# A graph layer and a mixture of experts on one core: thirteen experts' weights ahead instead of eleven, and a rearranged start and end of the expert loop

## The chip, the cores and the metric

The kernel runs on one core of a Trainium2 chip. Its time is the device time of one execution in microseconds (us), taken as the median of several runs; one further execution is recorded by the hardware profiler, and all views of the profile come from that one. Engines are named as the profile names them: PE (TensorE matmul), PEld (its weight load), DVE (VectorE), ACT (ScalarE), POOL (GpSimd) and SP (SyncE, which here only issues transfers). ACT and POOL issue transfers too.

## The reference

There are 1,024 nodes of 512 features, all in float32, and 16,384 edges sorted by target.

1. Graph layer: `x = x + relu(segment_sum(edge_weight * (layernorm(x) @ W)[src], dst) + bias)`.
2. Experts: `x' = layernorm(x)` is this layer's input; `scores = sigmoid(x' @ Wg.T + bg)`, and `nx` is `x'` normalised once more. The two best of 64 experts are taken, their scores divided by their sum.
3. Each expert computes `h = silu((nx*gamma_e + beta_e) @ W1_e + b1_e)`, times `(nx*gamma_e + beta_e) @ W3_e + b3_e` (512 to 256), then `h @ W2_e + b2_e` (256 to 512), weighted with the score. With W1, W3 and W2 an expert has three weight matrices of 524,288 B each, 64 experts together some 100 MB.
4. A shared expert of width 32 is applied to every node, and everything is added to `x`.

## The kernel before

**Graph stage.** The edges are turned into a dense matrix by one-hot matmuls (`one_hots`, `matrix_group`, `turn`), and `weighted_sum` (L507, 128 matmuls of 128x512) multiplies it with the normalised features times W. Tile by tile (8 tiles of 128 nodes) the stage normalises, stores the twice normalised rows to `nx_d` in device memory (`store_nx`, L539, on ACT's queue), transposes (`turn_x`), computes the scores (`scores`, L551, L554), takes the two best (`choose`, L560 to L572), counts each token's rank within its expert (`rank`, `put`, L588 to L598), and places token numbers in the lists of 32 pairs of experts with 64 places for each expert (`slots`, `listed`, L607 to L615). `lists` and `tokens` (L691, L692) come last.

**Blocks.** After that there are 33 blocks: one for every pair of experts (64 rows each), and at position 24 one overflow block for the tokens of an expert beyond its 64 places. Blocks are numbered 0 to 32 in the order they run. Each block does:

- `fetch`: POOL gathers 128 rows from `nx_d` (L717), up to four blocks ahead, in `NR` = 4 buffers that POOL zeroes first (L713);
- `front`: PE transposes them (L194), DVE applies gamma and beta (`scaled`, L729, L731);
- `hidden`: four bias matmuls (L742; b1 and b3 split into three bf16 terms, high and middle in `bias_hm`, low in `bias_lo`), sixteen matmuls with W1 and W3 (L746), Silu on ACT (L749), product on DVE (L751);
- `turned`: two transposes (L758) and a copy (L760);
- `back`, one block later: eight matmuls with W2 (`outputs`, L768), a copy on ACT (L771), and a scatter of 128 rows to `y_d` (L775, POOL).

The order of each engine's instructions is that of the program text (`manual_schedule`). Other work is put between the blocks: `beyond` and `beyond_list` work out the overflow block (blocks 2 to 11), and `other_rows`, `other_turn`, `other_sum` compute the shared expert and the b2 terms of one tile of nodes (L885 to L908): tiles 0 and 1 ahead of the loop, tiles 2 to 7 from block 13 on. `weights` (L791 to L798) normalises the scores and stores them to `w_d` (L795, on ACT's queue); it stands ahead of the loop.

**Weights.** `load_expert` issues W1, W3 (L703, L704, into one 8 KB slot per partition, tag `w13`) and W2 (L706, a 4 KB slot, tag `w2`) on SP's queue. There are `AHEAD` = 11 slots of each tag. The same slots serve the graph stage as temporary storage (`big` and `mid` tiles), and its end serves them again (`ys`, `bhots`, `diag`). Loads are issued in program order as slots come free. All transfers that SP and ACT issue share eight completion semaphores, taken in turn in the order of the program: a transfer waits on its queue until the one eight places ahead in that list has landed, whichever of the two queues that one is on.

**Pools.** The small tiles of the graph stage are in pools of their own (`gp`, `gp2`, `rt`); when these close, the pools of the blocks (`bp`, `gb`, `lp`, `psx`) take the same memory, and their first users wait for everything that used the closed pools.

**End.** When the scatter of block 31 has landed, eight loads (L1006, 512 KB each, alternately on ACT's and SP's queue) fetch `y_d`. The last block isn't scattered: PE adds its rows by one-hot matmuls (L1010), and one of the two rows of every odd tile by a diagonal matmul (L1012). DVE adds the rest (multiply-add L1014, sum L1016), and eight stores write the result (L1017).

The function and the loop around the change are these:

Of the kernel before, what the change touches and what calls it, by code (L numbers as in the profile page):

```python
# [18 lines left out]
P = 128  # L19
EPS = 1e-5  # L20
AHEAD = 11
# [3 lines left out]
def kernel(  # L25
# [111 lines left out]

    bias_hm = const.tile([P, 2 * H], BF16, name="bias_hm")
    bias_lo = const.tile([E, 2 * H], BF16, name="bias_lo")
    both = const.tile([P, E], BF16, name="both")  # L140
# [59 lines left out]
    with tc.tile_pool(name="graph", bufs=1) as gp, \  # L200
            tc.tile_pool(name="graph2", bufs=2) as gp2, \
# [5 lines left out]
        def row_tile(name):  # L207
            return gp2.tile([P, D], F32, name=name, tag="row", bufs=6)

        with tc.manual_schedule(engines={ENG.PE, ENG.DVE, ENG.Activation, ENG.Pool}):  # L210

            nc.gpsimd.iota(iota, pattern=[[1, P]], base=0, channel_multiplier=0, allow_small_or_imprecise_dtypes=True)
            thr_row = gp.tile([P, NH, P], F32, name="thr_row")
# [5 lines left out]
            diff = gp.tile([P, P], F32, name="diff")  # L219
# [32 lines left out]
            below = gp.tile([P, NH, P], BF16, name="below")  # L252
# [8 lines left out]
            rows = gp.tile([P, NH, EJ], I32, name="erows")  # L261
# [24 lines left out]
            def turn_h(i):  # L286
                pt = pst.tile([P, KC, P], F32, name="pt")
                transpose_rows(pt, hs.pop(i), P)
                hTs[i] = gp2.tile([P, KC, P], F32, name="hT")
                nc.scalar.copy(hTs[i], pt)  # L290
# [16 lines left out]
            sm = gp.tile([P, NH, EJ], F32, name="sm")  # L307
# [7 lines left out]
            d_w = gp.tile([P, NH, P], I32, name="d_w")  # L315
            s_w = gp.tile([P, NH, P], I32, name="s_w")
            e_w = gp.tile([P, NH, P], F32, name="e_w")
# [18 lines left out]
            b13 = mid([P, 2, H], "b13", F32)  # L336
            for n in range(2):
                nc.gpsimd.dma_start(b13[n * E:(n + 1) * E, 0, :], b1)
                nc.gpsimd.dma_start(b13[n * E:(n + 1) * E, 1, :], b3)
# [29 lines left out]
            blk_i = gp.tile([P, NH, P], I32, name="blk_i")  # L369
            nc.vector.tensor_scalar(blk_i, d_w, 2, None, op0=ALU.logical_shift_right)  # L370
            nc.vector.tensor_scalar(d_w, d_w, DL - 1, None, op0=ALU.bitwise_and)
            hi_i = gp.tile([P, NH, P], I32, name="hi_i")
            nc.vector.tensor_scalar(hi_i, s_w, 6, None, op0=ALU.logical_shift_right)
            nc.vector.tensor_scalar(s_w, s_w, LO - 1, None, op0=ALU.bitwise_and)
            part = gp.tile([P, 3, NH, P], F32, name="part")
# [39 lines left out]
            row_a = gp.tile([P, P], I32, name="row_a")  # L415
            nc.vector.tensor_scalar(row_a, at_i, 3, None, op0=ALU.logical_shift_right)
            nc.vector.tensor_scalar(row_a, row_a, 7, None, op0=ALU.bitwise_and)
            row_b = gp.tile([P, P], I32, name="row_b")
# [18 lines left out]
        with tc.If(unsure):  # L437
            for h in range(NH):
                nc.sync.dma_start(hw_d[h * D:(h + 1) * D, :].rearrange("(i p) d -> p i d", p=P), hws[h])
            bias_sb = row_tile("bias_sb")[:1, :]  # L440
            nc.sync.dma_start(bias_sb, gnn_bias[None, :])
# [4 lines left out]
            for b in range(NT // 2):  # L446
                node = row_tile("node")
# [27 lines left out]
        with tc.manual_schedule(engines={ENG.PE, ENG.DVE, ENG.Activation, ENG.Pool}):  # L475
# [35 lines left out]
            xts, xtTs, ohots, picked, ranks, earlier, bases, shifts = {}, {}, {}, {}, {}, {}, {}, {}  # L511
# [29 lines left out]
            def turn_x(t):  # L541
                pt = pst.tile([P, KC, P], F32, name="pt")
                transpose_rows(pt, xts.pop(t), P)
                xtTs[t] = gp2.tile([P, KC, P], F32, name="hT")
                nc.scalar.copy(xtTs[t], pt)

            def scores(t):
                pl = psh.tile([P, D], F32, name="ph")[:, :P]
                nc.tensor.matmul(pl, ones[0:1, :], brow, start=True, stop=False)
# [7 lines left out]
            def choose(t):  # L557
# [17 lines left out]
                earlier[t + 1] = to  # L575

# [8 lines left out]
            def put(t):  # L585
# [4 lines left out]
                odd_i = rt.tile([P, 2], U32, name="odd_i")  # L590
                nc.vector.tensor_scalar(odd_i, idx[:, t, :2], 1, None, op0=ALU.bitwise_and)
                pair_i = rt.tile([P, 2], U32, name="pair_i")
                nc.vector.tensor_scalar(pair_i, idx[:, t, :2], 1, None, op0=ALU.logical_shift_right)
                nc.vector.tensor_copy(pair[:, t, :], pair_i)
# [30 lines left out]
            def bias_terms():  # L625
                v = b13.rearrange("p a h -> p (a h)")
                terms = [mid([P, 2 * H], "bterm", BF16) for _ in range(2)]
                for term in terms:
                    nc.vector.tensor_copy(term, v)
                    nc.vector.tensor_sub(v, v, term)  # L630
# [28 lines left out]
            for t in range(NT + 4):  # L659
# [18 lines left out]
                if have(1):  # L678
                    turn_x(t - 1)
# [391 lines left out]
```

## Time and profile before

| | us |
|---|---|
| median of 3 runs | 466.25 |
| lowest, highest | 465.24, 466.73 |
| profiled execution, its time | 467.33 |
| profiled execution, its span | 465.5 |
| PE busy | 422.5 (91%) |
| DVE busy | 233.5 |
| POOL busy | 116.2 |
| ACT busy | 112.0 |
| moved by transfers | 132.48 MB, of which 107.56 on SP's queue |

The span is the stretch that the profiler saw; the time is that of the same execution as the runs are timed. Busy times are of the whole span and lump together stages with different limits, so they have to be read by stage. In a timeline the columns are start, duration, engine, line, operation, tiles (out<-in), count, and in brackets the idle time of the engine before it and what ended it. An engine's name with a q (SPq, ACTq) is the issue of a transfer.

### The profile page before, as it was taken

The numbers are of one execution on the slowest core, as the hardware profiler recorded it, in microseconds if no ns is written. First come the engines' busy times: TensorE is split into PE (matmuls) and PEld (weight loads), VectorE is DVE, ScalarE is ACT, GpSimd is POOL, SyncE is SP. The second block draws the span as 40 slices with busy tenths as digits, with TensorE's granted clock in tenths as the row PEclk, the third lists the DMA queues.
The fourth block names the chain that finished last, engine by engine and source line by source line (L and its number), as shares of the span: only waits on it lengthen the run. The fifth ranks groups of instructions, "written<-read, shape, count | busy, mean of one in ns | idle before, by whom it ended". The sixth has DMA issues, their size and how long they took to land. (4 is left out here: it accounts for less than half of the span.)

```text
span 465.5 us, 6433 instructions
## 1 busy us (share of the span) xinstructions
PE 422.5 (91%) x2182; PEld 210.6 (45%) x2182; DVE 233.5 (50%) x690; ACT 112.0 (24%) x240; POOL 116.2 (25%) x148
## 2 busy tenths in 40 slices
PE   2999999987999964996999999999999999999781
PEld 1554996754555543332434434333333443434230
DVE  6879996036877875428424333233233232412265
ACT  1335785324121212011111212112121121212200
POOL 6542200000432124312223233232232322200200
PEclk9999999998999985799899999999999999999988
DMA  8286830360786195359999999999999999999194
GB/s 263 87 121 102 321 130 3 125 259 28 244 316 204 52 375 195 121 194 410 356 389 407 407 407 406 407 408 405 408 404 409 406 405 407 405 410 403 47 366 174
DMA packets 42294, 132.48 MB, mean 285 GB/s; under 512 B 8023, under 2 KB 8151, under 8 KB 42128
## 3 DMA queue, kind: packets, MB, share of 16 engines
q1 hardware_dynamic: 30464, 107.56, 59.7%
q0 software_dynamic: 8304, 18.17, 13.3%
q10 hardware_dynamic: 3488, 6.30, 3.7%
q8 instruction: 18, 0.29, 0.3%
q14 instruction: 20, 0.16, 0.1%
HBM read 124.00 MB, written 18.88 MB: 307 GB/s over the span
## 5 line engine op out<-in xcount | busy, mean ns | idle before, releaser
L746 PE MATMUL xph<-w,xT 128*64 128x512 f32 (+1 forms) x520 | 126.5, 602 | 0.9 <-DMA w<-in_L_ffn_W_dram 0.9
L775 POOL DMA_INDIRECT y_d<-xy,lists x31 | 31.9, 1030 | 169.8 <-ACT xhT L760 70.4
L746 PEld LDWEIGHTS xph<-w,xT 128*64 128x64 f32 (+1 forms) x520 | 39.0, 138 | 66.6 <-issue 63.6
L768 PE MATMUL xpy<-w,xhT 128*64 128x512 f32 (+1 forms) x260 | 67.0, 593 | 0.6 <-ACT xhT L760 0.6
L751 DVE TENSOR_TENSOR xh<-xa,xph 128x256 f32<-128x256 f32 x33 | 13.9, 421 | 106.8 <-ACT xa L749 106.8
L507 PE MATMUL acc<-hw,AT 128*128 128x512 f32 x128 | 61.5, 607 | 0.0
L749 ACT ACTIVATE xa<-xph 128x256 f32<-128x256 f32 x33 | 12.6, 383 | 152.1 <-PE xph L746 152.1
L717 POOL DMA_INDIRECT rows<-nx_d,tokens x32 | 35.5, 1109 | 12.4 <-issue 9.1
L768 PEld LDWEIGHTS xpy<-w,xhT 128*64 128x64 f32 (+1 forms) x260 | 21.5, 138 | 37.2 <-issue 35.1
L485 PEld LDWEIGHTS ph<-oh 128*64 128x64 f32 x512 | 31.7, 212 | 5.7 <-issue 3.3
L485 PE MATMUL ph<-oh 128*64 128x64 f32 x512 | 33.3, 302 | 0.1
L297 PE MATMUL ph<-w_sb,hT 128*128 128x512 f32 x64 | 30.5, 625 | 0.7 <-ACT hT L290 0.7
L771 ACT COPY xy<-xpy 128x512 f32<-128x512 f32 x33 | 19.3, 586 | 49.0 <-PE xpy L768 44.1
L729 DVE TENSOR_TENSOR xT<-xpt,gT 128x512 f32<-128x512 f32 x32 | 22.0, 687 | 16.7 <-PE xpt L194 15.3
L507 PEld LDWEIGHTS acc<-hw,AT 128*128 128x128 f32 x128 | 22.3, 193 | 17.4 <-issue 17.4
L731 DVE TENSOR_TENSOR xT<-xT,bT 128x512 f32<-128x512 f32 x32 | 22.2, 693 | 1.1
L607 POOL TENSOR_SCALAR so<-rank_at,here 128x128 f32<-128x128 f32 x14 | 8.9, 634 | 54.5 <-DVE here L598 54.5
L194 PE MATMUL xpt<-ident,rows 128*128 128x128 f32 x132 | 22.3, 296 | 0.0
L401 DVE TENSOR_TENSOR oh<-eq,wt 128x1024 f32<-128x1024 bf16 x16 | 19.6, 1224 | 3.6 <-PE pt L498 2.2
L194 PEld LDWEIGHTS xpt<-ident,rows 128*128 128x128 f32 x132 | 19.5, 211 | 1.1 <-issue 0.6
L758 PEld LDWEIGHTS xpht<-ident,xh 128*128 128x128 f32 x66 | 11.8, 216 | 16.1 <-DVE xh L751 7.0
L297 PEld LDWEIGHTS ph<-w_sb,hT 128*128 128x128 f32 x64 | 12.4, 203 | 14.1 <-issue 13.1
(275 smaller groups left out, 493.9 us busy)
## 6 DMA issues: line engine op xcount, KB each, us to landing
w<-in_L_ffn_W_dram SPq DMA_DIRECT2D x195, 512.0 KB
y_d<-zero POOLq DMA_DIRECT2D x1, 4096.0 KB
base_d<-in_L_gnn_bias_dram POOLq DMA_DIRECT2D x1, 2048.0 KB, 19.9
base<-base_d POOLq DMA_DIRECT2D x8, 256.0 KB, 13.3
nx_d<-nx ACTq DMA_DIRECT2D x8, 256.0 KB
ys<-y_d ACTq DMA_DIRECT2D x4, 512.0 KB
ys<-y_d SPq DMA_DIRECT2D x4, 512.0 KB
w_sb<-in_L_gnn_W_dram ACTq DMA_DIRECT2D x1, 1024.0 KB
```

Of the source, the lines that this page charges most:

```text
L194: nc.tensor.transpose(ps[:, k, :], v[:, k, :], ident[:n, :n])
L297: nc.tensor.matmul(ph, hT[:, k, :], w_sb[:, k, :], start=(k == 0), stop=(k == KC - 1))
L401: nc.vector.tensor_tensor(oh[:, 1], eq[:, 1], wt[:, h, None, q].to_broadcast([P, LO, 16]), ALU.mult)
L485: nc.tensor.matmul(pa[LO * w:LO * (w + 1), u, :], oh[:, 1, :, q], oh[:, 0, :, q], start=True, stop=True)
L507: nc.tensor.matmul(accs[t], ATs[h][t // 4][:, t % 4, wq, :], hws[h][:, wq, :], start=(h == 0 and wq == 0), stop=(h == NH - 1 and wq == NQ ...
L717: nc.gpsimd.indirect_dma_start(out=rows, out_offset=None, in_=nx_d[:, :], in_offset=bass.IndirectOffsetOnAxis(ap=of, axis=0), bounds_check ...
L729: nc.vector.tensor_tensor(xT.rearrange(view, n=n), pt.rearrange(view, n=n), g[:, :, :, None].to_broadcast(over), ALU.mult)
L731: nc.vector.tensor_tensor(xT.rearrange(view, n=n), xT.rearrange(view, n=n), b[:, :, :, None].to_broadcast(over), ALU.add)
L746: nc.tensor.matmul(ph[n * r:(n + 1) * r], xT[:, k, n * r:(n + 1) * r], w13[:, :, k, :], start=False, stop=(k == KC - 1))
L768: nc.tensor.matmul(py[n * r:(n + 1) * r], hT[:, c, n * r:(n + 1) * r], w2[:, c, :], start=(c == 0), stop=(c == HC - 1))
L771: nc.scalar.copy(y, py)
L775: nc.gpsimd.indirect_dma_start(out=y_d[:, :], out_offset=bass.IndirectOffsetOnAxis(ap=numbers, axis=0), in_=y, in_offset=None, bounds_chec ...
```

## The change

- `AHEAD` goes from 11 to 13. The memory for it comes from the graph stage: its row tiles, turned tiles, early tiles and edge windows now lie in ring slots (`mid`, `big`), `beyond` keeps its tables in a `w2` slot (`room`), and several block tiles have fewer buffers (`xT` 2, `xa1`, `xh`, `xhT` and `st` 1, `xy` 2, `rows` 3).
- The bias is kept as three bf16 terms of 32 experts in one tile of 96 partitions per half (`bias3`, `picks`): a pair's block issues two bias matmuls instead of four. The tile is loaded by twelve small transfers on POOL instead of four.
- The blocks' pools wait tile by tile (`reuse_waits="tile"`), not for the whole closed pools.
- In the graph stage `score_bias` comes ahead of `turn_x`, and the two parity operations of `put` move to `choose`.
- The row buffers are zeroed by ACT. Three gathers are issued ahead of `front(0)`, the fourth after it.
- `weights()` moves from ahead of the loop to block 0, behind its `hidden`; the shared-expert work of all eight tiles moves into blocks 6 to 29.
- The last pair's loads come in the order W1, W3 of both experts, then W2 of both.
- The end: the last two blocks aren't scattered. The eight loads of `y_d` are all on SP's queue, directly behind the last weight loads. PE adds both blocks by one-hot matmuls, and the diagonal matmul is left for the last two tiles; the steps on DVE are in another order.

The core of the diff:

```diff
-AHEAD = 11
+AHEAD = 13
...
-    bias_hm = const.tile([P, 2 * H], BF16, name="bias_hm")
-    bias_lo = const.tile([E, 2 * H], BF16, name="bias_lo")
-    both = const.tile([P, E], BF16, name="both")
+    EH = E // 2
+    bias3 = const.tile([3 * EH, 2, 2 * H], BF16, name="bias3")
+    picks = const.tile([3 * EH, 2, E], BF16, name="picks")
...
-        def row_tile(name):
-            return gp2.tile([P, D], F32, name=name, tag="row", bufs=6)
+        row_ring = [pair[:, j] for pair in [mid([P, 2, D], "row", F32) for _ in range(3)] for j in range(2)]
+        turned_ring = mid([P, 2, KC, P], "hT", F32)
+        taken = {"row": 0, "turned": 0}
+        def row_tile(name=None):
+            taken["row"] += 1
+            return row_ring[taken["row"] % len(row_ring)]
+        def turned_tile():
+            taken["turned"] += 1
+            return turned_ring[:, taken["turned"] % 2]
...
-            b13 = mid([P, 2, H], "b13", F32)
-            for n in range(2):
-                nc.gpsimd.dma_start(b13[n * E:(n + 1) * E, 0, :], b1)
-                nc.gpsimd.dma_start(b13[n * E:(n + 1) * E, 1, :], b3)
+            b13 = mid([3 * EH, 2, 2, H], "b13", F32)
+            for n in range(3):
+                for a in range(2):
+                    for m, of in enumerate((b1, b3)):
+                        nc.gpsimd.dma_start(b13[n * EH:(n + 1) * EH, a, m, :], of[a * EH:(a + 1) * EH, :])
...
+            def score_bias(t):
+                pls[t] = psh.tile([P, D], F32, name="ph")[:, :P]
+                nc.tensor.matmul(pls[t], ones[0:1, :], brow, start=True, stop=False)
...
+                odds[t] = rt.tile([P, 2], U32, name="odd_i")
+                nc.vector.tensor_scalar(odds[t], idx[:, t, :2], 1, None, op0=ALU.bitwise_and)
+                pair_i = rt.tile([P, 2], U32, name="pair_i")
+                nc.vector.tensor_scalar(pair_i, idx[:, t, :2], 1, None, op0=ALU.logical_shift_right)
+                nc.vector.tensor_copy(pair[:, t, :], pair_i)
...
-                v = b13.rearrange("p a h -> p (a h)")
-                terms = [mid([P, 2 * H], "bterm", BF16) for _ in range(2)]
-                for term in terms:
-                    nc.vector.tensor_copy(term, v)
-                    nc.vector.tensor_sub(v, v, term)
-                nc.vector.tensor_copy(bias_hm[:E, :], terms[0][:E, :])
-                nc.vector.tensor_copy(bias_hm[E:, :], terms[1][E:, :])
-                nc.vector.tensor_copy(bias_lo, v[:E, :])
-                nc.vector.tensor_add(both, ident[:, :E], ident[:, E:])
+                terms = mid([3 * EH, 2, 2 * H], "bterm", BF16)
+                v = b13.rearrange("p a m h -> p a (m h)")
+                for n in range(3):
+                    part = slice(n * EH, (n + 1) * EH)
+                    nc.vector.tensor_copy(terms, v)
+                    nc.vector.tensor_copy(bias3[part], terms[part])
+                    if n < 2:
+                        nc.vector.tensor_sub(v, v, terms)
+                nc.vector.memset(picks, 0.0)
+                for n in range(3):
+                    part = slice(n * EH, (n + 1) * EH)
+                    for a in range(2):
+                        nc.vector.tensor_copy(picks[part, a, a * EH:(a + 1) * EH], ident[part, part])
...
+                    score_bias(t - 1)
...
-    bp = ctx.enter_context(tc.tile_pool(name="block", bufs=3))
-    gb = ctx.enter_context(tc.tile_pool(name="rows", bufs=1))
-    lp = ctx.enter_context(tc.tile_pool(name="late", bufs=1))
-    psx = ctx.enter_context(tc.tile_pool(name="ps_x", bufs=2, space=bass.MemoryType.PSUM))
-    def load_expert(queue, w1_of, w3_of, w2_of):
+    gb = ctx.enter_context(tc.tile_pool(name="rows", bufs=1, reuse_waits="tile"))
+    bp = ctx.enter_context(tc.tile_pool(name="block", bufs=3, reuse_waits="tile"))
+    lp = ctx.enter_context(tc.tile_pool(name="late", bufs=1, reuse_waits="tile"))
+    psx = ctx.enter_context(tc.tile_pool(name="ps_x", bufs=2, space=bass.MemoryType.PSUM, reuse_waits="tile"))
...
-    NR = 4
-    for rows in rows_of:
-        nc.gpsimd.memset(rows, 0.0)
+    NR = 3
...
-        for terms in (bias_hm, bias_lo):
-            rows = terms.shape[0]
+        for a in range(2):
             for n, (_, pick) in enumerate(parts):
-                nc.tensor.matmul(ph[n * r:(n + 1) * r], pick[:rows].to_broadcast([rows, r]), terms,
-                                 start=(terms is bias_hm), stop=False)
+                if a in pick:
+                    nc.tensor.matmul(ph[n * r:(n + 1) * r], pick[a].to_broadcast([3 * EH, r]), bias3[:, a, :],
+                                     start=(a == min(pick)), stop=False)
...
+        room = wpool.tile([P, 16, E], F32, name="room", tag="w2")
...
     with tc.manual_schedule(engines={ENG.PE, ENG.DVE, ENG.Activation, ENG.Pool, ENG.SP}):
-        for n in range(4):
+        for rows in rows_of:
+            nc.scalar.activation(rows, ones[:, 0:1].to_broadcast([P, D]), AF.Copy, scale=0.0)
+        for n in range(NR):
             fetch(n)
-        weights()
-        sts = [other_rows(i) for i in range(2)]
-        sTs = [other_turn(st) for st in sts]
-        for i in range(2):
-            other_sum(i, sTs[i])
         front(0)
+        fetch(NR)
         front(1)
         hots, st, sT = None, None, None
         for n, q in enumerate(order):
             if q < NP:
-                parts = [(load_expert(nc.sync, W1[e:e + 1], W3[e:e + 1], W2[e:e + 1]), both[:, e:e + 1])
-                         for e in (2 * q, 2 * q + 1)]
+                both = (2 * q, 2 * q + 1)
+                if n < LAST:
+                    experts = [load_expert(nc.sync, W1[e:e + 1], W3[e:e + 1], W2[e:e + 1]) for e in both]
+                else:
+                    experts = list(zip([load_first(nc.sync, W1[e:e + 1], W3[e:e + 1]) for e in both],
+                                       [load_second(nc.sync, W2[e:e + 1]) for e in both]))
+                parts = [(of, {e // EH: picks[:, e // EH, e:e + 1]}) for of, e in zip(experts, both)]
             else:
                 e = nc.values_load(oexp_i[0:1, 0:1], engines=[ENG.SP], min_val=0, max_val=E - 1)
-                parts = [(load_expert(nc.sync, W1[ds(e, 1)], W3[ds(e, 1)], W2[ds(e, 1)]), pick_o)]
+                parts = [(load_expert(nc.sync, W1[ds(e, 1)], W3[ds(e, 1)], W2[ds(e, 1)]), either)]
             fetch(n + 4)
+            if n == LAST:
+                y_of = y_d.rearrange("(i p n) d -> i p n d", p=P, n=2)
+                ys = [wpool.tile([P, 2, 2, D], F32, name="ys", tag="w13")[:, j] for i in range(NT // 2) for j in range(2)]
+                for i in range(NT):
+                    nc.sync.dma_start(ys[i], y_of[i])
+                hots_last = [block_hots(tokens[:, NP - 2 + m:NP - 1 + m], w_last[m]) for m in range(2)]
+                diag = wpool.tile([P, 2, P], F32, name="diag", tag="w2")
+                for j in range(2):
+                    nc.scalar.activation(diag[:, j, :], ident, AF.Copy, scale=wts[:, NT - 2 + j, 1:2])
             h = hidden(xTs.pop(n), parts)
-            back(n - 1)
+            if n < LAST:
+                back(n - 1)
+            else:
+                y_last = [outputs(*hTs.pop(LAST - 1))]
+            if n == 0:
+                weights()
             if n == 2:
                 beyond()
             if 4 <= n < 4 + NT:
             if n == 4 + NT:
                 beyond_lists()
-            if n >= 13 and (n - 13) // 3 + 2 < NT:
-                i = (n - 13) // 3 + 2
-                if n % 3 == 1:
+            if n >= 6 and (n - 6) // 3 < NT:
+                i = (n - 6) // 3
+                if n % 3 == 0:
                     st = other_rows(i)
-                elif n % 3 == 2:
+                elif n % 3 == 1:
                     sT = other_turn(st)
                 else:
                     other_sum(i, sT)
-            if n == LAST - 1:
-                w_last = block_weights(lists[:, NP - 1:NP])
-                hots_last = block_hots(tokens[:, NP - 1:NP], w_last)
-                diag = wpool.tile([P, NT // 2, P], F32, name="diag", tag="w2")
-                for i in range(1, NT, 2):
-                    nc.scalar.activation(diag[:, i // 2, :], ident, AF.Copy, scale=wts[:, i, 0:1])
+            if n == LAST - 2:
+                w_last = [block_weights(lists[:, NP - 2 + m:NP - 1 + m]) for m in range(2)]
             hTs[n] = (turned(h), parts)
             front(n + 2)
-        y_of = y_d.rearrange("(i p n) d -> i p n d", p=P, n=2)
-        queues = (nc.scalar, nc.sync)
-        ys = []
-        for i in range(NT):
-            ys.append(wpool.tile([P, 2, D], F32, name="ys", tag="w13"))
-            queues[i % 2].dma_start(ys[i], y_of[i])
-        y = outputs(*hTs.pop(LAST))
-        for i in range(NT):
-            po = psx.tile([P, D], F32, name=("xpt", "xph", "xpy")[i % 3])
-            nc.tensor.matmul(po, hots_last[:, i, :], y, start=True, stop=(i % 2 == 0))
-            if i % 2:
-                nc.tensor.matmul(po, diag[:, i // 2, :], ys[i][:, 0, :], start=False, stop=True)
-            for n in range(i % 2, 2):
+        pos = {}
+        def add_block(m, i):
+            if m == 0:
+                pos[i] = psx.tile([P, D], F32, name=("xpt", "xph", "xpy", "xpht")[i % 4])
+            nc.tensor.matmul(pos[i], hots_last[m][:, i, :], y_last[m], start=(m == 0), stop=(m == 1))
+            if m == 0 and i >= NT - 2:
+                nc.tensor.matmul(pos[i], diag[:, i - NT + 2, :], ys[i][:, 1, :], start=False, stop=False)
+        def add_rows(i):
+            for n in range(2 if i < NT - 2 else 1):
                 nc.vector.scalar_tensor_tensor(res[:, i, :], ys[i][:, n, :], wts[:, i, n:n + 1], res[:, i, :],
                                                op0=ALU.mult, op1=ALU.add)
-            nc.vector.tensor_add(res[:, i, :], res[:, i, :], po)
+        def add_sums(i):
+            nc.vector.tensor_add(res[:, i, :], res[:, i, :], pos.pop(i))
             queues[i % 2].dma_start(out[i * P:(i + 1) * P, :], res[:, i, :])
+        queues = (nc.scalar, nc.sync)
+        add_block(0, 0)
+        y_last.append(outputs(*hTs.pop(LAST)))
+        add_block(0, 1)
+        for i in range(2):
+            add_rows(i)
+        for i in range(NT):
+            add_block(1, i)
+            if i + 2 < NT:
+                add_block(0, i + 2)
+                add_rows(i + 2)
+            add_sums(i)
```

## The prediction

> **What bounds the kernel now.** I read the page's head first, then the waits of SP's queue, the issue rows on SP, the windows by stage, and the rows at the two joints: routing to block 0, and last block to the end.
>
> From the page:
>
> ```profile
> span 465.5 us, 6433 instructions
> ...
> PE 422.5 (91%) x2182; PEld 210.6 (45%) x2182; DVE 233.5 (50%) x690; ACT 112.0 (24%) x240; POOL 116.2 (25%) x148
> ...
> GB/s 263 87 121 102 321 130 3 125 259 28 244 316 204 52 375 195 121 194 410 356 389 407 407 407 406 407 408 405 408 404 409 406 405 407 405 410 403 47 366 174
> ```
>
> PE looks like the bound at 91%. But a slice is 11.6 us, and from slice 21 to slice 36 the transfers stand on a plateau of about 407 GB/s. The waits of the SP queue (line, what ended the wait, us in total, times, longest) say who is late:
>
> ```profile
> SPq L706 <- DMA w<-in_L_ffn_W_dram: 35.3, 36, 1.5
> ...
> SPq L703 <- DMA w<-in_L_ffn_W_dram: 32.9, 34, 1.4
> ...
> SPq L706 <- DMA nx_d<-nx: 23.0, 1, 23.0
> SPq L703 <- PE xph L746: 20.8, 1, 20.8
> ...
> SPq L1006 <- DMA y_d<-xy,lists: 17.7, 1, 17.7
> ```
>
> Weight loads wait for earlier weight loads. One waited 23.0 us for a store that ACT issued: a load on SP waits for whichever transfer, on SP or ACT, stands eight places ahead in one common list. And one waited 20.8 us for a matmul of block 0, a ring slot. Its place, and two windows (PE, PEld, DVE, ACT, POOL busy, granted PE clock, DMA share, GB/s):
>
> ```profile
> 172.91 0.33 SPq L706 DMA_DIRECT2D w<-in_L_ffn_W_dram  x1
> 194.91 0.33 SPq L703 DMA_DIRECT2D w<-in_L_ffn_W_dram  x1
> ```
>
> ```profile
> 180.00:195.00 15.00, 11.93 (x38) 5.56 (x38) 7.34 (x26) 2.21 (x6) 7.40 (x9) 0.63 0.23 59
> ...
> 260.00:420.00 160.00, 159.38 (x757) 64.95 (x758) 51.65 (x124) 28.95 (x76) 45.45 (x42) 1.00 1.03 407
> ```
>
> Eleven experts (33 tiles of 524,288 B) are issued by 172.91 and in by about 180.6; then the transfers idle until a slot comes free; from about 203 they carry 91.4 MB until the last weight byte at 432.7 (I call that time B). In 258.7 to 427.1, 120 tiles passed: 1.403 us each, with the gathers and scatters among them. PE itself waits for weights from 408 on. So the end is set by when the weight stream becomes continuous, by its length, and by the tail behind B, 465.5 - 432.7 = 32.8 us.
>
> **Routing to block 0.** The rows of the joint:
>
> ```profile
> 176.81 0.38 ACTq L795 DMA_DIRECT2D w_d<-wts  x1
> ...
> 178.97 0.32 DVE L885 TENSOR_SCALAR st<-iota,expert,wts 128x64 f32<-128x64 f32 x1 [1.59 <-DMA nx_d<-nx]
> ...
> 183.71 1.12 POOL L717 DMA_INDIRECT rows<-nx_d,tokens  x1 [2.46 <-DVE stt L887]
> ...
> 188.25 1.91 PE L194 MATMUL xpt<-ident,rows 128*128 128x128 f32 x8
> 190.10 0.64 PE L742 MATMUL xph<-bias_hm,both 128*64 128x512 bf16 x2
> ...
> 191.23 3.65 PE L746 MATMUL xph<-w,xT 128*64 128x512 f32 x16
> ```
>
> The tile wait takes away DVE's 1.59 us behind a store; four DVE steps of other outputs (0.32 + 0.31 + 0.28 + 0.28 = 1.2 us) leave the chain, and two small operations per tile move ahead of the rank. I count 2.9 us: token numbers at 180.0 instead of 182.9 (bounds 179.6 and 180.6). The first gather follows 0.8 us later, at 180.85, and lands 3.2 us after that, at 184.1, as the row of before does. The four POOL fills (2.03 us, ended 181.25) were not on this path; as three ACT operations they aren't either. PE's two L907 steps (3.62 us up to 188.46) are gone from in front of the transposes, so block 0's bias starts at about 187.0 (second gather's rows at 185.5, then transposes), 3.1 us earlier.
>
> PE then runs at half clock: in the trace the granted clock is 0.50 from 184.5 to 191.0 and 1.00 from 191.5, some 6.7 us after unbroken work began. After, work begins at 184.3, so full clock comes near 191; 7.5 of the sixteen L746 steps go at 0.456 us, the rest at 0.228 (3.65 / 16): block 0's hidden ends at 192.9 instead of 194.9. The Trainium skill, "TensorE: Matmul & The Clock Gate", Part 1 (the clock gate), puts the release after about 4 us of sustained matmuls; by it this stage would end some 1.3 us sooner, and the whole kernel with it. The row decides, and 190.9 to 194.0 are my bounds.
>
> **The store that moves, and the wait it makes.** The store of the pair weights (w_d) goes from 176.81 to behind block 0's Silu on ACT. On ACT only the copies of block 0 stand behind it. On SP the case is different: in the list of after it stands eight places ahead of expert 9's w1, so that load waits for its landing, and the other 167 loads are queued behind that load. 27 tiles (experts 0 to 8) are ahead instead of 33, and the two added slots can't be filled early. Hidden ends 192.9, Silu 0.38, product 0.42, four weight operations 0.92 (from 175.86 to 176.78 before), hops 0.2: issue at 194.8. Before, its 1,024 packets of 8 B ran from 2.2 to 4.2 us after issue, beside weights; landing is signalled 0.3 to 0.6 us after the last packet (scatter and row store of the joints). So expert 9 is issued at X = 199.2; bounds 197 (idle queues, faster block 0) and 203 (packets slower, clock later). The Trainium skill, "DMA: Bandwidth & Descriptors", Anatomy of one DMA, gives a DMA a fixed cost of about 2.0 us; by that X would be about 197. No row shows this store alone.
>
> From X on the ring never empties the queue: twelve tiles find free slots at once (16.8 us), and by 216 blocks 0 to 2 have given theirs back. So 168 tiles, 88.1 MB, and 7.4 MB of gathers and scatters go at 406.9 GB/s: 234.7 us, and 1.2 us from issue to first bytes. B = 199.2 + 1.2 + 234.7 = 435.1, against 432.7: the stream ends 2.4 us LATER. The earlier start of block 0 and the wider ring don't pay, but the ring-limited stretch (391 GB/s from 205, 369 from 220) is gone, which gives back most of the six missing tiles (8.4 us).
>
> **Bias.** Two bias matmuls for a pair instead of four: 0.335 us less (303.17, 303.50, 303.84 are consecutive starts), 32 times, 10.7 us of PE. Two more tiles of other outputs in the loop add 1.9. PE alone would be done near 421, 14 us ahead of the stream: 187.0, the first 27 blocks as before (190.10 to 390.08, 200.0) less 27 x 0.335, plus 1.9, six blocks of 6.55, and 2 for the last output. So I cost this at nothing; were PE the bound it would be worth 8.8. The longer splitting on DVE lies in its idle stretch 80 to 100; eight more bias loads on POOL (0.52 each, 4.2 us) push the first base loads to 54, needed at 100.6: nothing, or 1 us if POOL is tighter than it looks. Graph tiles in ring slots: the weight loads wait there for the graph stage as before, in stretches that PE bounds; I take zero, 1 us either way.
>
> **The tail.** The rows of before:
>
> ```profile
> 441.02 2.05 ACTq L1006 DMA_DIRECT2D ys<-y_d  x4
> 441.05 1.98 SPq L1006 DMA_DIRECT2D ys<-y_d  x4
> ...
> 445.81 1.54 DVE L1014 SCALAR_TENSOR_TENSOR res<-ys,wts,res 128x512 f32<-128x512 f32 x2 [8.95 <-DMA ys<-y_d]
> ...
> 460.00 0.69 DVE L1016 TENSOR_TENSOR res<-res,xph 128x512 f32<-128x512 f32 x1
> ```
>
> Blocks are numbered 0 to 32. The reload of y waits for the scatter of block 31 (issued 438.34, packets until 440.68): B + 8.3. DVE starts 4.8 us later and works 14.9 us without a gap; 4.8 us of output store follow. After, blocks 31 and 32 stay on chip, and the reload needs only the scatter of block 30, which follows the hidden step of block 31 and is issued at about B - 1.9 (430.57 before); with 2.7 us to landing (438.34 to 441.02) the reload goes out at about B + 1.3. All on one queue, the first tile lands alone, in 3.7 us: DVE starts at B + 5.0. If that scatter takes the 5.2 us to first packets that the one at 422.75 took amid weights, B + 7 to B + 8. DVE does 14 multiply-adds of 0.77 and 8 sums of 0.70, 16.4 us instead of 14.9 (two odd rows move back from PE). Block 32's output is copied near B + 8.4 and PE adds it by B + 9.4, while DVE is on tile 2. End B + 5.0 + 16.4 + 4.8 = B + 26.2, against B + 32.8: 6.6 us less.
>
> **Sum.** 435.1 + 26.2 = 461.3, against a span of 465.5: 4.2 less. The profiled execution took 467.33, 1.83 more than its span, and lies 1.08 above the median of 466.25. So 461.3 + 1.83 - 1.08 = 462.05; I say 462.0.
>
> **Rivals.**
>
> *The store's wait eats the tail (slower).* Every us of X past 199.2 is a us of end: no gain from X = 203.4, slower than can be told (0.3%, 1.4 us) from 204.8. For: a load has waited 23.0 us for a store of ACT before, this one has 1,024 packets where a row store has 128, and each step ahead of it is on half clock. Against: the same store took about 5 us amid full traffic. X = 207 gives 470.
>
> *The tail doesn't shorten.* The scatter of block 30 lands amid weights and the reload's first tile comes at B + 8: end B + 29.2, time 465.
>
> *The wait isn't there or is short (faster).* If loads run on at 180.6, 162 tiles and 7.4 MB end by 408 and PE becomes the bound at 421; then the bias saving counts in full, and with about 18.5 us from last output to end the time is 440 to 450. Against it: the list position, and the 23.0.
>
> **How the numbers follow.** My forecast (458 to 466) gets 0.54, the slower rival 0.21, the unchanged tail 0.13, the faster one 0.12. Bounds: X -2 to +4, tail -1.5 to +3, graph stage 1 either way, rate 0.5% of 235 us, 1.2. The range goes on to 452, where the wait is half gone, and to 469, where X is 206; left out are the core of the faster rival (0.10) and the slower one's far side (0.08). Below 464.85: 0.64; within 0.3%: 0.13; above 467.65: 0.23.
>
> **What would show it.** Right: a gap on SP's queue from about 173 to about 199 that ends on w_d's landing; then 407 GB/s without the dip at 220 to 240; last weights near 435 with PE idle in most blocks from the twelfth on; DVE's first end step 5 us behind the last weights. Wrong: a weight load between 181 and 194 (faster rival); X past 203; PE without idle time in the last blocks, which would make the bias matmuls count; a reload issued more than 5 us behind B.

## The result, and the profile after

The changed kernel takes 468.36 us (median of 20 runs, 465.22 to 469.64), the kernel before 466.41 us (20 runs, 465.08 to 468.60). The ratio is 1.0031, 95% interval 1.0017 to 1.0046: slower by 0.3%. I had forecast 4.2 us faster. The profiled execution of the changed kernel took 467.19 us with a span of 465.4, 0.1 us less than that of before, so the two traces show most of what went wrong, and the runs show the rest.

The page of the changed kernel (span, busy times, GB/s in 40 slices):

```profile
span 465.4 us, 6337 instructions
...
PE 420.5 (90%) x2130; PEld 212.3 (46%) x2130; DVE 241.2 (52%) x709; ACT 113.3 (24%) x241; POOL 116.9 (25%) x153
...
GB/s 274 76 121 90 217 256 2 345 18 45 249 316 239 168 92 72 34 308 413 407 407 406 408 406 408 407 407 410 406 408 408 407 408 405 407 409 410 264 340 114
```

Counted from 0, slices 14 to 16 are emptier than before (92, 72 and 34 against 375, 195 and 121), the plateau begins in slice 18, and it reaches into slice 37 (264 against 47). The waits of SP's queue say why:

```profile
SPq L724 <- DMA w<-in_L_ffn_W_dram: 56.5, 53, 2.6
...
SPq L730 <- DMA nx_d<-row: 37.5, 2, 28.4
...
SPq L723 <- DMA w_d<-wts: 23.7, 1, 23.7
...
SPq L1005 <- DMA y_d<-xy,lists: 9.5, 1, 9.5
```

The wait for the slot (20.8 us before) is gone, and one of 23.7 us for the store of w_d stands in its place. The joint, in the timeline:

```profile
174.80 0.33 SPq L730 DMA_DIRECT2D w<-in_L_ffn_W_dram  x1
...
181.97 1.12 POOL L742 DMA_INDIRECT rows<-nx_d,tokens  x1 [5.09 <-issue]
...
185.32 1.98 PE L193 MATMUL xpt<-ident,rows 128*128 128x128 f32 x8 [4.67 <-DMA rows<-nx_d,tokens]
...
187.96 4.52 PE L771 MATMUL xph<-w,xT 128*64 128x512 f32 x16
...
194.19 0.38 ACTq L821 DMA_DIRECT2D w_d<-wts  x1
...
198.87 0.33 SPq L723 DMA_DIRECT2D w<-in_L_ffn_W_dram  x1
```

The 28th tile (expert 9's W1) leaves SP at 198.87, when the store of 194.19 has landed. The windows of this trace (PE, PEld, DVE, ACT, POOL busy, clock, DMA share, GB/s) show the stage that follows:

```profile
180.00:195.00 15.00, 9.24 (x40) 4.78 (x41) 4.83 (x14) 0.74 (x3) 5.39 (x6) 0.68 0.16 45
...
220.00:240.00 20.00, 20.00 (x96) 7.77 (x94) 6.91 (x19) 3.07 (x7) 5.63 (x5) 0.90 1.03 407
...
260.00:420.00 160.00, 152.36 (x681) 62.20 (x677) 50.63 (x123) 28.91 (x77) 41.67 (x40) 1.00 1.03 407
```

The dip at 220 to 240 (369 GB/s before) is filled, and PE is idle 7.6 us between 260 and 420 where it was idle 0.6. The end:

```profile
435.07 1.03 POOL L800 DMA_INDIRECT y_d<-xy,lists  x1 [4.16 <-ACT xhT L785]
...
438.28 3.73 SPq L1005 DMA_DIRECT2D ys<-y_d  x8
...
441.46 2.99 DVE L1050 SCALAR_TENSOR_TENSOR res<-ys,wts,res 128x512 f32<-128x512 f32 x4 [1.50 <-DMA ys<-y_d]
...
445.50 1.54 DVE L1050 SCALAR_TENSOR_TENSOR res<-ys,wts,res 128x512 f32<-128x512 f32 x2 [1.05 <-DMA ys<-y_d]
...
457.38 1.02 PE L1044 MATMUL xpy<-xy,bhots 128*128 128x512 f32 x2
...
458.44 0.69 DVE L1054 TENSOR_TENSOR res<-res,xpy 128x512 f32<-128x512 f32 x1 [1.89 <-PE xpy L1044]
```

The last weight byte comes at 437.4, DVE starts 4.1 us behind it, and near the end it waits 1.89 us for PE.

### The profile page after: what moved, and what is told of

Same layout as the page of the kernel before. It is cut to its first block, busy times and chain, and to the rows that moved or that the text cites. A ratio compares the mean times of both kernels' runs of the same rounds, so it can differ in the third digit from the quotient of the medians.

```text
span 465.4 us, 6337 instructions
## 1 busy us (share of the span) xinstructions
PE 420.5 (90%) x2130; PEld 212.3 (46%) x2130; DVE 241.2 (52%) x709; ACT 113.3 (24%) x241; POOL 116.9 (25%) x153
## 4 chain that ended last, share of the span: by engine, by line
DMA 49%; PE 33%; DVE 4%; issue 2%; ACT 1%; POOL 0%; SPq 0%; ACTq 0%; POOLq 0%; DVEq 0%
DMA w<-in_L_ffn_W_dram 47%; PE acc L514 11%; PE ph L492 7%; PE xph L771 4%; PE pt L505 2%; PE xpy L793 2%; PE ph L563 1%; DMA w_d<-wts 1%; PE pt L193 1%; PE xpt L1044 1%; PE xph L1044 1%; PE xpht L1044 1%; PE xpy L1044 1%; DMA rows<-nx_d,tokens 1%; DVE bnst L166 0%
## 5 line engine op out<-in xcount | busy, mean ns | idle before, releaser
L771 PE MATMUL xph<-w,xT 128*64 128x512 f32 (+1 forms) x520 | 136.3, 605 | 8.0 <-DMA w<-in_L_ffn_W_dram 7.9
L771 PEld LDWEIGHTS xph<-w,xT 128*64 128x64 f32 (+1 forms) x520 | 44.2, 140 | 77.7 <-issue 72.0
L793 PE MATMUL xpy<-w,xhT 128*64 128x512 f32 (+1 forms) x260 | 74.3, 593 | 0.0
L793 PEld LDWEIGHTS xpy<-w,xhT 128*64 128x64 f32 (+1 forms) x260 | 23.7, 138 | 37.0 <-issue 33.4
L742 POOL DMA_INDIRECT rows<-nx_d,tokens x32 | 34.1, 1067 | 24.1 <-issue 14.9
```

The costliest lines, as they stand in the source:

```text
L742: nc.gpsimd.indirect_dma_start(out=rows, out_offset=None, in_=nx_d[:, :], in_offset=bass.IndirectOffsetOnAxis(ap=of, axis=0), bounds_check ...
L771: nc.tensor.matmul(ph[n * r:(n + 1) * r], xT[:, k, n * r:(n + 1) * r], w13[:, :, k, :], start=False, stop=(k == KC - 1))
L793: nc.tensor.matmul(py[n * r:(n + 1) * r], hT[:, c, n * r:(n + 1) * r], w2[:, c, :], start=(c == 0), stop=(c == HC - 1))
```

## The experiments

**Theories.** *Stream*: the end follows the last weight byte, which follows X, the time at which the first load behind the gap is issued. *PE*: PE, 90% busy, is the bound. Times are medians, and ratios are to the kernel before, which had 466.28 to 466.75 in the same rounds. In what was expected, the theory and its rival stand side by side.

**The changed kernel again** (`again`), no edit.

> The changed kernel as it is, for a second trace and as the measure of the others on the same chip. Stream theory (the end follows the last weight byte, and the weight stream starts when the store of w_d has landed): first load behind the gap at 198 to 201, last weight byte 238.5 us later, 437 to 440, end 28 us behind that; time 466 to 470, and where the span is longer than 465.4 the gap's end is later by as much. PE theory (PE, 90% busy, is the bound): the span does not follow the gap's end.

Measured: 468.16, ratio 1.0028 (0.9999 to 1.0057); X 198.89, span 466.0, 267.1 us behind X. It confirms the first trace and settles no theory.

**The store taken out of the list** (`store_pool`):

```diff
-        nc.scalar.dma_start(w_d.rearrange("(i p n) o -> p i (n o)", p=P, n=2), wts)
+        nc.gpsimd.dma_start(w_d.rearrange("(i p n) o -> p i (n o)", p=P, n=2), wts)
```

> The store of w_d is issued by POOL instead of ACT, at the same place; it then is no part of the list of transfers that SP's loads wait on. Stream theory: no load waits for it; loads run on from about 175 through 39 tiles as slots allow, the list ends some 13 to 15 us sooner, last weight byte 422 to 425 instead of 437.4, end 28 us behind it: span 450 to 453, time 452 to 455 (3% below the changed kernel). PE theory: PE's work is the same, so time 465 to 469, no different from the changed kernel.

Measured: 459.93, ratio 0.9858 (0.9832 to 0.9885): 8.2 us below the changed kernel. The PE theory falls. But I had expected 13 to 15, and the trace shows where the rest is. A window, and the first transposes of block 0:

```profile
185.00:195.00 10.00, 4.95 (x16) 2.56 (x18) 2.68 (x4) 0.00 (x0) 3.63 (x4) 0.50 0.87 330
```

```profile
190.05 2.10 PE L193 MATMUL xpt<-ident,rows 128*128 128x128 f32 x8 [8.20 <-DMA rows<-nx_d,tokens]
```

While the transfers, weights for the most part, move 330 GB/s, the first gather (issued 183.18) is followed by transposes only 6.9 us later; it was 3.4 in the gap (181.97, 185.32). Block 0 is 4.8 us late, and every slot that it gives back with it.

**The store ahead of block 0 again** (`store_early`):

```diff
             fetch(n)
+        weights()
         front(0)
...
-            if n == 0:
-                weights()
```

> The pair weights and their store on ACT stand ahead of front(0) again, as in the kernel before; the store stays in the list. Stream theory: issued near 182, landed near 187, so the gap ends at 187 instead of 198.9; last weight byte 425 to 427, span 453 to 455, time 455 to 457, and block 0 up to 0.9 us later for the four DVE steps ahead of it. PE theory: no gain, 466 to 470.

Measured: 458.94, ratio 0.9850 (0.9811 to 0.9889), 9.2 us below the changed kernel, and yet longer than the 455 to 457 expected. The store was issued at 177.5, earlier than I had thought (182). SP's queue:

```profile
174.79 0.33 SPq L730 DMA_DIRECT2D w<-in_L_ffn_W_dram  x1
181.89 0.33 SPq L723 DMA_DIRECT2D w<-in_L_ffn_W_dram  x1
...
203.75 0.33 SPq L730 DMA_DIRECT2D w<-in_L_ffn_W_dram  x1
```

The gap splits: 7 us for the store, then 15 us (from 188.65) at expert 12's W2, which waits for the outputs of block 0. So the place of the store costs 8 to 9 us, shown in two ways.

**The bias matmuls doubled** (`bias_twice`):

```diff
-        for a in range(2):
+        for a in (0, 1, 2, 3):
             for n, (_, pick) in enumerate(parts):
-                if a in pick:
+                if a % 2 in pick:
...
-                                     start=(a == min(pick)), stop=False)
+                                     start=(a % 2 == min(pick)), stop=(a < 2 and a == max(pick)))
```

> The changed kernel with its bias matmuls issued twice (the first pass is overwritten by the second): four per pair block as before the change, so PE has 0.335 us more in each of 32 blocks, 10.7 us. Stream theory: hidden in PE's idle time, 0 to 1 us more than the changed kernel. PE theory: 8 to 11 us more, 477 to 479.

Measured: 469.18 against 468.16, 1.0 us for 10.7 us of PE work (ratios to before 1.0048 and 1.0028, intervals overlapping). PE's waits for weights in the changed kernel, and in this one:

```profile
PE xph L771 <- DMA w<-in_L_ffn_W_dram: 7.9, 11, 1.1
```

```profile
PE xph L771 <- DMA w<-in_L_ffn_W_dram: 5.8, 9, 1.0
```

PE's busy time between 260 and 420 rises by only 1.9 us (152.36 to 154.23) though 34 more matmuls stand in it, and the waits above fall by 2.1: most of the added work goes into pauses that these views count as busy or don't list. It isn't all hidden: in this trace X is 197.83 and the span 465.9, 268.1 behind X, 1 us or more above the traces with single bias (266.4 to 267.1). The bias saving is worth about 1 us of its 10.7 while the stream sets the end.

**The end of before** (`old_end`): load order of the last pair, scatter of block 31, reload on two queues, the single block on chip and four diagonal matmuls as they were.

```diff
-            if n < LAST:
-                back(n - 1)
-            else:
-                y_last = [outputs(*hTs.pop(LAST - 1))]
+            back(n - 1)
...
+        queues = (nc.scalar, nc.sync)
+        for i in range(NT):
+            queues[i % 2].dma_start(ys[i], y_of[i])
+        y = outputs(*hTs.pop(LAST))
```

> The changed kernel with the end of the kernel before: loads of the last pair in the old order, block 31 scattered, the reload of y behind that scatter on two queues, one block added by one-hot matmuls, diagonal matmul for four tiles. Theory of the forecast: the new end was worth 6.6 us, so 475. Theory of the traces (32.7 us from last weight byte to end before, 28.0 after): 4 to 5 us, so 472 to 473. Rival (the end is bound by something both have in common, the 4.2 MB reload and the output stores): under 1.5 us.

Measured: 472.03, ratio 1.0116 (1.0084 to 1.0147), 3.9 us above the changed kernel. Its span is 272.0 us behind X (469.3, X 197.32), that of the changed kernel 266.4 to 267.1. The new end gains 3.9 us in the runs and 5.3 by this distance, not 6.6: the theory of the traces holds.

**Eleven slots with the early store** (`early_11`):

```diff
-AHEAD = 13
+AHEAD = 11
```

> The store of w_d ahead of front(0), and eleven slots of each tag instead of thirteen. Theory: with the wait gone the two slots carry six more tiles before the first slot comes free, 6 x 1.40 = 8.4 us of stream, less what ring-limited issue gives back; 462 to 466, 4 to 7 us more than with thirteen. Rival (the table of beyond() in the W2 ring, which makes expert 12's W2 wait for the outputs of block 0, limits both alike): under 2 us more, 459 to 461.

Measured: 467.55, ratio 1.0013 (0.9994 to 1.0032), 8.6 us above the same with thirteen, where I had expected 4 to 7. The two slots are worth what six tiles take (8.4) once they can be filled; in the changed kernel they can't be. The run says one thing more: with the slots of before and the new end it is no faster than the kernel before (466.75). Its last weight byte comes at 435.6, where the two traces of before have 432.8 and 429.9. Something else in the change delays the stream by about as much as the new end gains; no run takes that apart.

**The table of beyond() in the other ring** (`early_room`):

```diff
-        room = wpool.tile([P, 16, E], F32, name="room", tag="w2")
+        room = wpool.tile([P, 2, KC, H], F32, name="room", tag="w13")
+        room = room[:, 0].rearrange("p k (a e) -> p (k a) e", e=E)
```

> The store of w_d ahead of front(0), and the table of beyond() in a slot of the W1/W3 ring instead of the W2 ring. In the trace with the early store the loads stop again from 189 to 203.8, at expert 12's W2, which waits for the outputs of block 0. Theory: that load now goes out with the hidden step of block 0 (about 195) and the stream ends 4 to 8 us sooner: 451 to 455. Rival: the next load (expert 13's W1) waits for a block just as long, and the gain is under 2 us: 457 to 459.

Measured: 458.61, ratio 0.9820 (0.9795 to 0.9844), which overlaps that of the early store alone. In its trace block 0's bias comes at 193.49 (191.29 with the early store alone). The theory's gain did not come, and the time is in the rival's range: the next load (expert 12's W1) did go out with block 0's hidden step, but this ends at 199.8 only (192.48 in the changed kernel). The first gather, issued at 183.15 beside weights, is followed by transposes at 190.66.

**PE kept busy ahead of block 0** (`warm_pe`, four matmuls; `warm_ident`, twenty small ones that read only the identity):

```diff
+        idle = psx.tile([P, D], F32, name="xpy")
+        for _ in range(4):
+            nc.tensor.matmul(idle, ident, wall.rearrange("p k h -> p (k h)")[:, :D], start=True, stop=True)
         front(0)
```

> The changed kernel with four matmuls of 128x512 into an unused bank ahead of block 0's transposes, so that PE is busy from 180.7 instead of 185.3. Theory: the granted clock goes to 1.00 near 188 instead of near 190, block 0's hidden ends 1 to 2 us sooner, the store of w_d and the gap's end with it, and the time by the same: 466 to 467, with less spread between executions. Rival (the clock of this stretch does not matter): 468 as the changed kernel, or 0 to 1 us more where the four matmuls delay the transposes.

Measured: 471.97, ratio 1.0107 (1.0083 to 1.0132), 3.8 us slower. The edit did something else than meant. ACT's timeline:

```profile
186.94 1.15 ACT L979 ACTIVATE rows<-ones 128x512 f32<-128x512 f32 x2 [9.04 <-PE xpy L984]
```

Row buffers lie in memory of the tile that the added matmuls read, so their zeroing waited, and the second gather with it. By accident it moves X. Its first load behind the gap:

```profile
203.34 0.33 SPq L723 DMA_DIRECT2D w<-in_L_ffn_W_dram  x1
```

X is 4.5 us later, the span (469.7) 4.3 us longer, 266.4 behind X. Block 0's bias came 4.0 us later too (191.27), so this run alone would fit the PE theory as well; `store_pool`, where block 0 came later and the end sooner, doesn't.

```diff
+        for _ in range(20):
+            nc.tensor.matmul(idle[:, :P], ident, ident, start=True, stop=True)
```

> The changed kernel with twenty matmuls of 128x128 ahead of block 0's transposes. They read the identity alone, which stays where it is through the whole kernel; those of the run before read a graph-stage tile whose memory the row buffers take, and held up the zeroing of two of these (ACT idle 9.04 us behind them) and with it the second gather by 4.4 us. Theory: PE busy from 180.7 on, granted clock 1.00 near 188, block 0's hidden 1 to 2 us sooner, the gap's end at 197 to 198, span 463.5 to 464.5, time 466 to 467.5, less spread. Rival (the clock there does not move the end): 467.5 to 469.

Measured: 468.88, ratio 1.0059 (1.0039 to 1.0080): no gain. The clock was at 1.00 from 184 on, but block 0's hidden ended at 192.28 instead of 192.48: the transposes began 1.1 us later behind the added matmuls (186.41), and hidden then waited for DVE. The time is in the rival's range, but the run does not part the two: from the first transpose to the end of hidden it took 5.9 us instead of 7.2, so the clock saved 1.3 us there and the added matmuls cost 1.1 ahead of it. What the half clock costs without that delay was not tried.

**Four more traces** (`look_1` to `look_3` of the changed kernel, `look_before`), no edit.

> The changed kernel once more, for a trace of an execution near its median. Theory: executions differ by where the graph stage and block 0 end (clock), the gap's end X follows, and the span is X + 266.5 (as in the three traces so far: 266.5, 267.1, 266.4 with the disturbed gather). Rival: X is 198 to 199 as before and a longer span is lost behind it, in the stream or in the tail.

> As look_1: span X + 266.5 by the theory; a longer rest by the rival.

> As look_1: span X + 266.5 by the theory; a longer rest by the rival.

> The kernel before once more. Its profiled execution took 467.33, its median is 466.4: theory: this trace is nearer 464.6 in span, shorter by as much as block 0 starts earlier than 190.1, since its loads up to 252 wait for slots that the blocks give back.

Measured: spans 465.6, 465.2 and 463.3 with X at 198.93, 198.37 and 196.75: 266.7, 266.8 and 266.6 behind X, as the theory has it. None of these executions is as slow as the median (468.36), so X there is inferred. The shortest one's first load behind the gap:

```profile
196.75 0.33 SPq L723 DMA_DIRECT2D w<-in_L_ffn_W_dram  x1
```

The second trace of the kernel before has a span of 463.0, and its block 0 begins like this:

```profile
187.63 0.41 PE L742 MATMUL xph<-bias_hm,both 128*64 128x512 bf16 x2
```

That is 2.5 us earlier than in the trace I forecast from (190.10), with a span shorter by the same 2.5. Executions of either kernel differ ahead of the loop. The quick trace of each kernel is the one without a dip of the granted clock in the middle of the graph stage. The window 100 to 110 of the first and the second trace of before:

```profile
100.00:110.00 10.00, 7.41 (x24) 3.79 (x23) 5.83 (x21) 3.37 (x4) 0.54 (x1) 0.83 0.25 93
```

```profile
100.00:110.00 10.00, 7.41 (x31) 4.06 (x30) 7.44 (x26) 3.70 (x6) 0.54 (x1) 1.00 0.21 70
```

For the changed kernel's first trace and `look_3` the same window has 0.89 and 1.00. Among traces with a dip the order is another: in `old_end` the window has 0.83, and block 0's bias starts at 185.86, ahead of the 187.24 of the first trace. So the clock of this window is at most part of the cause, and no run tried it.

**All stores on POOL** (`all_pool`, `all_pool_room`): the row stores too, and then the table of beyond() moved as above.

```diff
-                nc.scalar.dma_start(nx_d[t * P:(t + 1) * P, :], nx)
+                nc.gpsimd.dma_start(nx_d[t * P:(t + 1) * P, :], nx)
...
-        nc.scalar.dma_start(w_d.rearrange("(i p n) o -> p i (n o)", p=P, n=2), wts)
+        nc.gpsimd.dma_start(w_d.rearrange("(i p n) o -> p i (n o)", p=P, n=2), wts)
```

> The stores of w_d and of the rows (nx_d) are all issued by POOL: SP's weight loads then wait for slots and for their own kind alone. Theory (in the run with w_d alone on POOL, block 0 started at 192.1 instead of 187.2 because the gathers shared the engines with weights from 176 to 192): more tiles are in before 176, the gathers meet fewer of them, block 0 starts at 188 to 190, and the end comes 2 to 6 us ahead of that run: 454 to 458. Rival (row stores on POOL delay the lists and gathers, which POOL makes too): block 0 later than 192 and 460 to 463.

Measured: 458.75, ratio 0.9839 (0.9814 to 0.9863), some 1 us below the run with w_d alone on POOL. Block 0's bias is back at 187.09 (192.08 there), as the theory has it, but the time is just past the range I gave: expert 12's W2 still waits for the outputs of block 0, to 200.69.

> The same with the table of beyond() in a slot of the W1/W3 ring. Theory: expert 12's W2 no longer waits for the outputs of block 0 (near 204), and the transfers stand still 4 to 8 us less: 449 to 455. Rival (as with the early store, block 0 is later by what the gathers lose to weights): no more than 1 us from the run before.

Measured: 454.61, ratio 0.9753 (0.9720 to 0.9786), at the upper end of the range. The queue of SP:

```profile
175.82 0.33 SPq L730 DMA_DIRECT2D w<-in_L_ffn_W_dram  x1
192.88 0.33 SPq L723 DMA_DIRECT2D w<-in_L_ffn_W_dram  x1
```

The loads of twelve experts are issued by 175.8, and expert 12's W1 goes out with block 0's hidden step. This version is 2.5% faster than the kernel before.

## Why the prediction was wrong

**Right.** The gap at expert 9's w1, its cause and its end: X 199.2 forecast, 198.87 measured; block 0's bias at 187.0, measured 187.24; hidden ended 192.9, measured 192.48; the store issued 194.8, measured 194.19. The ring-limited dip is gone, the bias saving is hidden but for about 1 us, PE idles in the later blocks. The slower rival had the right place, and its price of 1:1 holds over X from 196.75 to 203.34: the span was X + 266.4 to X + 267.1 in all seven traces with the new end, single bias and the store behind block 0 on ACT's queue.

**Right in part by luck.** The steps to X were off in both directions. The first gather went out at 181.97, not 180.85, and its rows came at 185.32, not 184.1; full clock came near 190, not 191. The landing of the store, 4.4 us after issue in the forecast and 4.7 in the trace, is the plainest case. I took the packets to end 4.2 us after issue and the landing to follow by 0.3 to 0.6. The packets ended after 1.6 us, and the landing followed 3.1 later. The trace of before had a sign of this. There a matmul ahead of block 0 waited for the same store:

```profile
183.23 0.50 PE L900 MATMUL xpt<-ident,st 128*97 128x128 f32 x1 [0.75 <-DMA w_d<-wts]
```

That is 6.4 us after issue (176.81), 2.2 behind the last packet, and not "about 5". In the seven traces the store held the load for 4.4 to 5.0 us.

**Wrong: the sum that this wait was weighed against.** I put break-even at X = 203.4. The median of before, 466.41, stands for a span of 464.6 (the profiled runs are 1.8 us longer than their spans), and 464.6 - 266.7 = 197.9. The wait as I forecast it was already past break-even. Three terms failed.

*The stream's length, B = X + 235.9.* It took 238.5 us (198.87 to 437.4). I divided all bytes by the plateau rate, but the stream neither starts nor stops at it. The last window of the changed kernel:

```profile
434.50:437.40 2.90, 2.90 (x15) 1.63 (x16) 2.79 (x12) 1.16 (x4) 1.03 (x1) 1.00 0.42 164
```

From 198.87 to 201.1 it ran at 102 and 188 GB/s, and in the last 2.9 us at 164. The trace of before had it in plain view (201 GB/s from 430.0 to 432.8). The stream was 2.6 us longer than I had it; with X 0.3 early, B was 2.3 late.

*The tail, 26.2 us.* It took 28.0 (437.4 to 465.4). The reload went out at B + 0.9 and DVE started at B + 4.1, both better than I said, and DVE's work was 15.3 us, not 16.4. But it waited 3.3 us that I had not counted: 1.05 for the reload's third tile, the rest for PE, whose sixteen one-hot steps and two diagonal ones follow each other every 0.86 us: I had costed the first of them and left PE out of the rest of the tail. The last output store took 5.4 instead of 4.8. From trace to trace the tail is 4.7 us shorter (32.7 to 28.0). The rival of the unchanged tail did not come. For it I took 5.2 us to the first packets of the scatter at 422.75; its packets ran from 4.2 to 5.3.

*The execution I counted from.* Block 0 at 190.10 was a late execution of before. By its own distance to the median (1.08) my forecast stands for X = 199.2 - 1.08 = 198.1 in a median execution; the changed kernel's median, 468.36, stands for a span of 466.55 and X = 199.9 (by 266.7; no trace of such an execution was taken). That is 1.8 us. The earlier start of block 0 is smaller than 3.1 between like executions: 185.02 in the quickest trace after, 187.63 in the quicker of before, 2.6.

Together 2.6 + 1.8 + 1.8 = 6.2, which is what lies between -4.2 and +1.95. The first two terms are measured; the third rests on the medians.

**What the change does.** Two slots of each tag (8.6 us when they can be filled), a shorter end (4) and an earlier block 0 stand against a store that keeps the slots empty (8.2 to 9.2); and the kernel before had 33 tiles in ahead of its own gap, this one 27. These parts do not add up to the 0.3%: by `early_11` the rest of the change costs some 5 us (467.55 - 466.75 + 3.9, if the end is worth the same there), and which part of it does is open. The faster rival's price is answered too: without the wait the time is 459 to 460, not 440 to 450, since expert 12's W2 and the gathers became late next.

Of the Trainium skill, "TensorE: Matmul & The Clock Gate", Part 1, the 4 us fit this time: the clock was 0.50 up to 189 and 1.00 from 190 with PE busy from 185.32. In the trace of before it took 6.7, in `warm_ident` some 2.7 (0.69 in 182 to 184 with PE busy from 180.60). The page says that the window runs freely, so one trace is a poor measure of it. The fixed 2.0 us of "DMA: Bandwidth & Descriptors", Anatomy of one DMA, which that section gives for transfers that GpSimd issues, did not fit the store of w_d on ACT's queue: it landed 4.7 us after issue.

What stays open: why executions differ by some 4 us, for the most part ahead of the loop, what delays the stream in `early_11`, and how the 8.6 us of the slots share out between tiles that are in early and the ring-limited stretch.

## What to carry to other kernels

When a store moves, look for what waits for it in the order of completion, not only for who reads it: a transfer of 8 KB on ACT's queue held 88 MB on SP's. A wait that is seen and priced correctly must still be weighed against gains that are measured from the same kind of execution; add up a stream from its first byte to its last, with its slow ends, and a tail for every engine in it. Where one event sets the end, plot span against it over a few executions: here seven traces gave a constant within 0.7 us, and with it the break-even.

## What the runs showed of the hardware

The store of w_d (1,024 packets of 8 B) was issued at 194.19 and its last packet was over by 195.8 in the trace's packet records, yet the load that waited for it went out at 198.87, 3.1 us after the last packet (in `again` 1.8 us, 4.4 after issue); a row store of 256 KB issued at 172.69 in the same trace let the load behind it go at 174.80, 2.1 us later. A gather of 128 rows lengthens from 3.4 to 6.9 us, issue to first transpose, when weights run beside it and the transfers together move 330 GB/s.
